# Statistics and pooled sums of the next image, done in three parts between the tap blocks instead of in one piece after them

## The chip, the cores and the metric

The program runs on one core of one Trainium2 chip. The metric is the device time of one execution in microseconds (us). The engines are PE (TensorE: matrix products and transposes), DVE (VectorE), ACT (ScalarE), POOL (GpSimd) and SP (SyncE, which issues the DMAs). Each engine works through its own queue in order; an instruction that must wait holds up everything behind it in that queue. PE writes its results to PSUM, in tiles named `ps`; ACT and DVE read them out.

## The reference

Four blocks follow one another on a batch x of 32 images with 192 channels of 56 by 56 points, in float32. Each normalises x over groups of 6 channels, applies a layer, and adds the result to x. Layer 0 is an agent attention, layer 1 a two-way recurrent scan, layer 2 a shifted 3 by 3 blur, and layer 3 a convolution as large as the image. The change lies in the kernel's attention stage, so layer 0 is what matters:

```python
qkv = xf @ Wqkv + bqkv                       # x normalised, all 3136 points
agent = qi.mean(axis=(2, 4))                 # q averaged over 8 by 8 points: 49 agents
agent_attn = softmax(ah * scale @ kh + pos_bias)      # over the points
agent_v = agent_attn @ vh
q_attn = softmax(qh * scale @ ah + agent_bias)        # over the 49 agents
out = q_attn @ agent_v + dwc(vh)             # dwc: a 3 by 3 convolution per channel
x = x + out @ proj_w + proj_b
```

The normalisation needs the mean and the variance of each group of channels over the whole image. The agents need only the sums of x over squares of 8 by 8 points, because the mean of q is a product of the mean of x.

## The kernel before

The program runs in stages. First a filter for layer 3 is made, up to about 230 us. Then the attention takes the images one after another, up to about 4850 us; the scan follows up to about 8200 us, and the channel stage (layers 2 and 3) ends the program.

An image is held as two tiles: `x[0]` has channels 0 to 127, with all 56 rows, and `x[1]` has channels 128 to 191, with the upper half of the rows on partitions 0 to 63 and the lower half on 64 to 127. Its points are cut into four blocks of columns, numbered 0 to 3, of 16, 16, 16 and 8 columns (`WIDTHS`). The attention of one image (from line 843) has two parts.

The first loop runs over the blocks j. `weigh(j)` multiplies the block with the agents' keys in three steps of two heads each; DVE takes the maximum of each (`low`, L664), ACT the exponential of it (`pr`, L666). `turn_v(j)` and `turn(j)` transpose the values and the weights on PE (L681, L694), and ACT copies the results (`vT` L682, `prT` L697). `gather(j - 1)` multiplies the turned weights of the block before with its values (L709), and `settle` turns and adds that block's result (L718 on PE, `got` L720 on ACT and L722 on DVE). `find_v(j + 2)` computes the values of a later block (L621 to L634). `convolve(j + 1)` computes the 3 by 3 convolution of the next block: ACT starts it (L647) and DVE adds eight taps for each of the two tiles (L649). Behind the last block, `moments` of the next image runs in the place of a convolution.

The second part starts with `ask(0)`: PE multiplies the first block with the agents' queries (L763, L764), DVE takes maxima (`mx`, L767) and subtracts them (`pq`, L768), ACT takes exponentials (L776), DVE sums and divides (L778 to L780). `join` (L727 to L742) merges the four blocks' softmaxes into `values`. The second loop, over t, asks for the other blocks, turns the weights back (L790), answers (L801, L806), projects (L921 to L934) and adds to x (L816, L822). Between these steps it prepares the next image: `spread_of` (with the matrix product L545) and `scaling` finish the statistics, `normed`, `find_v(0)`, `find_v(1)`, `find_agents`, `seen` and `convolve(0)` follow.

`moments` (L510 to L539) is all DVE work: seven `bn_stats` of `x[0]` (L515), four of `x[1]` (L517), two aggregates (L519, L520), sums over 8 columns of both tiles (`by_x`, L524), and sums over 8 rows (`pool_a` L527; `fours` L532 and `pool_c` L535).

The order of each engine's queue is not the order of the code. A planner takes the instructions of the program in the order in which they are written as their priority, follows a model of their durations, and puts into each engine's queue whatever can start by that model; so an instruction written early goes early, and later ones fill holes. `psum()` hands out four result tiles. The images lie in two buffers; the next image's load (L424, L426) is issued when the image before has been stored.

Of the kernel before, what the change touches and what calls it, by code (L numbers as in the profile page):

```python
# [23 lines left out]
ALU = mybir.AluOpType  # L24
AX = mybir.AxisListType
# [17 lines left out]
POOL = 7  # L43
# [396 lines left out]
def attention(ctx: ExitStack, tc: tile.TileContext, a, ready, x1, st_a, st_c, beside):  # L440
# [9 lines left out]
    nc = tc.nc  # L450
# [11 lines left out]
    def psum():  # L462
        return pp.tile([128, 2, BANK], F32, name="ps", tag="ps")
# [30 lines left out]
    def small(name, shape):  # L494
        return sp.tile(shape, F32, name=name, tag=name)
# [14 lines left out]
    def moments(x):  # L510

        st_a, st_c = small("st_a", [128, 7, 6]), small("st_c", [128, 4, 6])
        flat = [t.rearrange("p y x -> p (y x)") for t in x]
        for i in range(7):
            nc.vector.bn_stats(st_a[:, i], flat[0][:, i * 448 : (i + 1) * 448])  # L515
        for i in range(4):
            nc.vector.bn_stats(st_c[:, i], flat[1][:, i * 392 : (i + 1) * 392])  # L517
        mv = small("mv", [128, 2, 2])
        nc.vector.bn_aggr(mv[:, 0], st_a.rearrange("p a b -> p (a b)"))  # L519
        nc.vector.bn_aggr(mv[:, 1], st_c.rearrange("p a b -> p (a b)"))  # L520
        pool_a, pool_c = small("pool_a", [128, AG]), small("pool_c", [65, AG])
        by_x = [wp.tile([128, n, POOL], F32, name="by_x", tag=f"by_x{n}", bufs=1) for n in (S, S // 2)]
        for t in range(2):
            nc.vector.tensor_reduce(  # L524
                by_x[t].rearrange("p y q -> p (y q)"), x[t].rearrange("p y (q x) -> p (y q) x", x=8), AX.X, ALU.add
            )
        nc.vector.tensor_reduce(  # L527
            pool_a.rearrange("p (w q) -> p w q", w=POOL), by_x[0].rearrange("p (w y) q -> p w q y", y=8), AX.X, ALU.add
        )
        fours = small("fours", [64, 2 * POOL, POOL])  # L530
        for h, r in HALVES:
            nc.vector.tensor_reduce(  # L532
                fours[:, h * POOL : (h + 1) * POOL], by_x[1][r].rearrange("p (w y) q -> p w q y", y=4), AX.X, ALU.add
            )
        nc.vector.tensor_tensor(  # L535
            pool_c[0:64].rearrange("p (w q) -> p w q", w=POOL), fours[:, 0::2], fours[:, 1::2], ALU.add
        )
        nc.vector.memset(pool_c[64:65], 1.0)
        return mv, (pool_a, pool_c)  # L539

    def grouped(src):
        ps = psum()
# [5 lines left out]
    def spread_of(mv):  # L548

        mean = small("mean", [128, 2])  # L550
        nc.vector.tensor_copy(mean, grouped([mv[:, t, 0:1] for t in range(2)]))
        d = small("d", [128, 2])
        nc.vector.tensor_tensor(d, mv[:, :, 0], mean, ALU.subtract)
        nc.vector.tensor_tensor(d, d, d, ALU.mult)
        nc.vector.tensor_tensor(d, d, mv[:, :, 1], ALU.add)
        return mean, d

    def scaling(mean, d, pools):

        pool_a, pool_c = pools  # L560
        rs, nb = small("rs", [128, 2]), small("nb", [128, 2])
        nc.vector.tensor_scalar(rs, grouped([d[:, t : t + 1] for t in range(2)]), GN_EPS, None, ALU.add)
        nc.scalar.activation(rs, rs, AF.Ln)
        nc.scalar.activation(rs, rs, AF.Exp, scale=-0.5)
        nc.vector.scalar_tensor_tensor(nb, mean, -1.0, rs, ALU.mult, ALU.mult)
        rs64 = small("rs64", [128, 2])
        nc.vector.tensor_scalar(rs64, rs, 1.0 / (S // POOL) ** 2, None, ALU.mult)
        nc.vector.tensor_scalar(pool_a, pool_a, rs64[:, 0:1], nb[:, 0:1], ALU.mult, ALU.add)
        nc.vector.tensor_scalar(pool_c[0:64], pool_c[0:64], rs64[0:64, 1:2], nb[0:64, 1:2], ALU.mult, ALU.add)
        return rs, nb  # L570
# [83 lines left out]
    def weigh(j, g, low, sums):  # L654
        _, n, _ = sizes(j)
        prs = []
        for p in range(3):
            cols = slice(p * PAIR, (p + 1) * PAIR)
            ps = psum()
            for h in range(2):  # L660
                px = slice(h * n, (h + 1) * n)
                mm(ps[P2, h, :n], g[:, cols], xs_a[j][:, px], start=True, stop=False)  # L662
                mm(ps[P2, h, :n], gk_c[0:KC, 2 * j + h, cols], xs_c[j][0:KC, px], start=False, stop=True)  # L663
            nc.vector.tensor_reduce(low[:, j, p : p + 1], ps[P2, :, :n], AX.XY, ALU.max, negate=True)  # L664
            pr = wp.tile([PAIR, 2, CH], F32, name="pr", tag="weights", bufs=WB)
            nc.scalar.activation(  # L666
                pr[:, :, :n], ps[P2, :, :n], AF.Exp, bias=low[:, j, p : p + 1], accum_out=sums[:, j, p : p + 1]
            )
            prs.append(pr)
        return prs  # L670
# [43 lines left out]
    def settle(j, halves, got):  # L714

        ps = psum()
        for p in range(3):
            nc.tensor.transpose(ps[P2, 0, p * 128 : (p + 1) * 128], halves[:, p * PAIR : (p + 1) * PAIR], ident)  # L718
        both = ps[P2, 0, : 3 * 128].rearrange("p (a h d) -> p a h d", a=3, h=2)
        nc.scalar.copy(got[:, j].rearrange("p (a d) -> p a d", a=3), both[:, :, 0])  # L720
        mine = got[:, j].rearrange("p (a d) -> p a d", a=3)
        nc.vector.tensor_tensor(mine, mine, both[:, :, 1], ALU.add)  # L722
# [109 lines left out]
            )  # L832

    nxt = ready.first
    mv, pools = moments(nxt)
    rs, nb = scaling(*spread_of(mv), pools)
    ag = find_agents(0, pools)
    gk = seen(ag, wkT, gk_c, "gk_a")
# [4 lines left out]
    for b in range(NB):  # L843
        x, more = nxt, b + 1 < NB
        if more:
            nxt = ready.image(nc, a, b + 1)
        beside(b)
        low, sums = small("low", [PAIR, NK, 3]), small("sums", [PAIR, NK, 3])
        got = sp.tile([PAIR, NK, C], F32, name="got", tag="got", bufs=1)
        turned, asked, back = {}, {}, {}  # L850
        for j in range(NK):
            prs = weigh(j, gk, low, sums)
            if j == 0:
                gq = seen(ag, wqT, gq_c, "gq_a")
            vT = turn_v(j, v[j])
            if j > 0:
                halves = gather(j - 1, *turned[j - 1])
            if j + 2 < NK:
                v[j + 2] = find_v(j + 2)
            turned[j] = turn(j, prs), vT  # L860
            if j > 0:
                settle(j - 1, halves, got)
            if j + 1 < NK:
                o[j + 1] = convolve(j + 1)
            elif more:
                mv, pools = moments(nxt)
        halves = gather(NK - 1, *turned[NK - 1])
        asked[0] = ask(0, gq)
        settle(NK - 1, halves, got)
        values = join(low, sums, got)  # L870
        done, o = o, {}
        st = small("st", [128, 2, 9])
        for t in range(1, NK + 2):
            if t < NK:
                asked[t] = ask(t, gq)
            if more and t == 1:
                mean, d = spread_of(mv)
            if more and t == 2:
                rs, nb = scaling(mean, d, pools)
                normed(nxt, rs, nb, 0)  # L880
            if t <= NK:
                back[t - 1] = turn_back(t - 1, asked[t - 1])
            if more and t in (3, 4):
                v[t - 3] = find_v(t - 3)
            if t >= 2:
                project(t - 2, done[t - 2], x, st)
            if t <= NK:
                answer(t - 1, back[t - 1], values, done[t - 1])
            if more and t == 2:
                ag = find_agents(b + 1, pools)  # L890
                normed(nxt, rs, nb, 1)
            if more and t == 3:
                gk = seen(ag, wkT, gk_c, "gk_a")
                normed(nxt, rs, nb, 2)
            if more and t == 4:
                o[0] = convolve(0)
                normed(nxt, rs, nb, 3)
        nc.sync.dma_start(out=st_a[:, b % 2, b // 2], in_=st[:, 0])
        for h, r in HALVES:
            nc.sync.dma_start(out=st_c[b % 2, :, h, b // 2], in_=st[r, 1])  # L900
        nc.sync.dma_start(out=x1[b, 0:128], in_=x[0].rearrange("p y x -> p (y x)"))
        for h, r in HALVES:
            nc.sync.dma_start(
                out=x1[b, 128:C, 1568 * h : 1568 * h + 1568], in_=x[1][r].rearrange("p y x -> p (y x)")
            )
# [1094 lines left out]
```

## Time and profile before

| what | us |
|---|---|
| median of three runs | 10493.24 (10483.27 to 10510.5) |
| profiled execution: its time, its span | 10489.98, 10488.2 |
| PE busy over the span | 9430.8 (90%) |
| DVE busy | 9115.9 (87%) |
| ACT busy | 6351.2 (61%) |
| POOL busy | 2225.9 (21%) |
| mean granted PE clock | 0.963 of full speed |

A busy time counts the engine's own instructions, not the waits between them, and the share is an average over stages that have different limits. PE's busy times are modelled at their ends and overlap a little; the granted clock says what share of full speed PE was allowed. In a row of the timeline the first number is the start in us from the span's start and the second the length; `low<-ps` says that `low` is written from `ps`, `x2` counts instructions in the row, and `[2.88 <-PE ps L764]` says that the engine was idle for 2.88 us before it, until a PE instruction of line 764 released it. Lines are those of the kernel before.

### The profile page before, as it was taken

The page shows a single profiled execution, that of the slowest core. Times are in us where ns is not written, and L with a number is a line of the kernel's source. Part 1 is how long each engine was busy: PE and PEld are TensorE (multiplying, and loading weights), DVE is VectorE, ACT ScalarE, POOL GpSimd, SP SyncE. Part 2 cuts the span into 40 slices and gives each one's busy share as a digit, 9 for nine tenths or more (in the row PEclk, how much of TensorE's full clock was granted, in tenths as well). Part 3 has the DMA queues.
Part 4 walks back from the last instruction along what each step waited for, and adds up shares of the span by engine and source line. Part 5 has one row for each costly group of instructions (what it writes and reads, how often), then busy time and mean ns, then how long its engine had stood idle before and what let it go on. Part 6 is the DMA issues. An engine that isn't in the chain of part 4 may idle for free. (4 is left out here: it accounts for less than half of the span.)

```text
span 10488.2 us, 163343 instructions
## 1 busy us (share of the span) xinstructions
PE 9430.8 (90%) x63814; PEld 5820.0 (55%) x63814; DVE 9115.9 (87%) x11284; ACT 6351.2 (61%) x11964; POOL 2225.9 (21%) x1751
## 2 busy tenths in 40 slices
PE   5999999999999999998888888888888798999998
PEld 3556555555555555554333333433433587787776
DVE  5888888888888888887999999999999687888887
ACT  3555555555555555554666666666666476777776
POOL 0000000000000000000433333333333444444441
PEclk8999999999999999999899999999999899999999
DMA  4211222122211211011344444444444599999999
GB/s 127 67 42 59 67 67 66 37 65 67 67 49 52 67 49 49 27 46 57 87 106 101 100 100 102 104 104 105 106 100 102 145 285 273 286 292 284 281 286 281
DMA packets 1111098, 1247.63 MB, mean 119 GB/s; under 512 B 773091, under 2 KB 813440, under 8 KB 1098232
## 3 DMA queue, kind: packets, MB, share of 16 engines
q1 hardware_dynamic: 1089388, 1209.08, 40.6%
q10 hardware_dynamic: 20932, 28.02, 1.0%
q8 instruction: 507, 8.31, 0.3%
q14 instruction: 271, 2.22, 0.1%
HBM read 916.15 MB, written 306.43 MB: 117 GB/s over the span
## 5 line engine op out<-in xcount | busy, mean ns | idle before, releaser
L649 DVE SCALAR_TENSOR_TENSOR o<-v_a,att_w,o 128x896 f32<-128x896 f32 (+1 forms) x1024 | 1058.7, 1034 | 423.5 <-ACT v_a L623 303.3
L1167 POOL MEMSET f<- 128x2 f32 x48 | 4.5, 100 | 4738.4 <-DMA st_c<-st 4735.9
L1546 ACT COPY y<-ps 64x252 f32<-64x252 f32 (+1 forms) x2304 | 785.9, 341 | 105.9 <-PE ps L1546 76.3
L1546 DVE STREAM_TRANSPOSE z<-turned 128x1792 f32<-128x1792 f32 x192 | 677.1, 3527 | 161.9 <-ACT turned L1546 161.2
L1161 ACT ACTIVATE pq<-pq 128x784 f32<-128x784 f32 x384 | 330.0, 860 | 673.3 <-DVE pq L1157 673.0
L1157 DVE SCALAR_TENSOR_TENSOR pq<-both,eu,pq 128x1568 f32<-128x1568 f32 x384 | 702.2, 1843 | 2.0 <-POOL f L1156 0.4
L1153 DVE TENSOR_TENSOR_SCAN pq<-decay,f,both 128x784 f32<-128x784 f32 x384 | 695.8, 1841 | 8.4 <-ACT both L1183 8.4
L666 ACT ACTIVATE pr<-ps,low 98x896 f32<-98x896 f32 (+1 forms) x384 | 352.9, 919 | 572.0 <-DVE low L664 572.0
L1153 DVE TENSOR_TENSOR_SCAN pq<-decay,b,both 128x784 f32<-128x784 f32 x384 | 694.7, 1842 | 0.0
L921 PE MATMUL ps<-x,weights 128*128 128x392 f32 x1536 | 585.6, 520 | 90.3 <-ACT x L1141 63.7
L649 DVE SCALAR_TENSOR_TENSOR o<-v_c,att_w,o 128x448 f32<-128x448 f32 (+1 forms) x1024 | 640.1, 625 | 5.1
L662 PE MATMUL ps<-xs_a,gk_a 128*98 128x448 f32 (+1 forms) x1536 | 637.0, 496 | 0.0
L663 PE MATMUL ps<-xs_c,gk_c 125*98 125x448 f32 (+1 forms) x1536 | 631.2, 492 | 0.0
L776 ACT ACTIVATE pq<-pq 128x1176 f32<-128x1176 f32 (+2 forms) x224 | 242.3, 1082 | 634.2 <-DVE pq L768 612.2
L1141 ACT ACTIVATE x<-x,nb,rs 128x784 f32<-128x784 f32 x384 | 387.7, 1033 | 339.7 <-DMA x<-x 178.6
L763 PE MATMUL ps<-gq_a,xs_a 128*128 128x294 f32 (+1 forms) x1600 | 544.8, 423 | 37.7 <-DVE pq L768 33.1
L1546 PEld LDWEIGHTS ps<-toep,y 128*32 128x32 f32 x16896 | 500.4, 150 | 137.5 <-ACT y L1546 130.8
L1546 POOL TENSOR_TENSOR xn<-x,scale 128x896 f32<-128x896 f32 x192 | 327.2, 1704 | 1099.3 <-DMA x<-x 563.0
L1156 POOL COPY b<-pq 128x2 f32<-128x2 f32 x192 | 419.0, 2182 | 660.5 <-DVE pq L1153 567.1
L1546 PE MATMUL ps<-toep,y 128*32 128x112 f32 x16896 | 547.5, 285 | 2.0 <-DMA toep<-spans 2.0
L1546 PE MATMUL ps<-rows,xn 128*112 128x112 f32 x3072 | 366.6, 275 | 193.2 <-POOL xn L1546 192.2
L764 PE MATMUL ps<-gq_c,xs_c 125*128 125x294 f32 (+1 forms) x1600 | 517.8, 411 | 0.0
(360 smaller groups left out, 23528.0 us busy)
## 6 DMA issues: line engine op xcount, KB each, us to landing
toep<-spans SPq DMA_DIRECT2D x192, 2352.0 KB
x<-x SPq DMA_DIRECT2D x576, 392.0 KB
x<-x SPq DMA_DIRECT2D x896, 196.0 KB
out_x<-done SPq DMA_DIRECT2D x384, 196.0 KB
spans<-lags SPq DMA_DIRECT2D x24, 2352.0 KB
x<-in_x SPq DMA_DIRECT2D x32, 1568.0 KB
x<-x SPq DMA_DIRECT2D x32, 1568.0 KB
gq_c<-once SPq DMA_DIRECT2D x32, 821.1 KB
```

The source lines that it names most:

```text
L649: nc.vector.scalar_tensor_tensor(dst, tap(i), dww[:, t, i : i + 1], dst, ALU.mult, ALU.add)
L662: mm(ps[P2, h, :n], g[:, cols], xs_a[j][:, px], start=True, stop=False)
L663: mm(ps[P2, h, :n], gk_c[0:KC, 2 * j + h, cols], xs_c[j][0:KC, px], start=False, stop=True)
L666: nc.scalar.activation(pr[:, :, :n], ps[P2, :, :n], AF.Exp, bias=low[:, j, p : p + 1], accum_out=sums[:, j, p : p + 1])
L763: mm(ps[:m, k - q, :HA], xs_a[j][:, px], g, start=True, stop=False)
L764: mm(ps[:m, k - q, :HA], xs_c[j][0:KC, px], gq_c[0:KC, which[k]], start=False, stop=True)
L921: mm(out, aa, srcs[t][h], start=True, stop=False)
L1141: nc.scalar.activation(xs[t], xs[t], AF.Identity, bias=nb1[:, t, s.p : s.p + 1], scale=rs1[:, t, s.p : s.p + 1])
L1153: nc.vector.tensor_tensor_scan(to, decay[:, of(t)].to_broadcast([128, MC]), data, at[:, i : i + 1], ALU.mult, ALU.add)
L1156: nc.gpsimd.tensor_copy(at, z[:, :, last])
L1157: nc.vector.scalar_tensor_tensor(before, both, eu[:, of(t)], before, ALU.mult, ALU.add)
L1546: return lambda *args, **kw: self.tc.keep_in_program_order(do(*args, **kw))
```

## The change

`moments` becomes a generator with three parts, and the image loop takes one part at a time. The first part holds the seven `bn_stats` of `x[0]`. The second holds the four of `x[1]`, both aggregates, and the pooled sums of `x[1]` (small `by_x`, `fours`, `pool_c`). The third holds the pooled sums of `x[0]` (large `by_x`, `pool_a`). For j = 1, 2 and 3 one part is written behind block j's `settle(j - 1)` and ahead of `convolve(j + 1)`, where there is one. At j = 0 the generator is only made and nothing runs. For the first image, before the loop, all parts run at once as before. The instructions are the same ones; in the last image, which has no successor, there are none, as before.

```diff
         for i in range(7):
             nc.vector.bn_stats(st_a[:, i], flat[0][:, i * 448 : (i + 1) * 448])
+        yield
         for i in range(4):
             nc.vector.bn_stats(st_c[:, i], flat[1][:, i * 392 : (i + 1) * 392])
...
-        for t in range(2):
+
+        def by_column(t):
             nc.vector.tensor_reduce(
                 by_x[t].rearrange("p y q -> p (y q)"), x[t].rearrange("p y (q x) -> p (y q) x", x=8), AX.X, ALU.add
             )
-        nc.vector.tensor_reduce(
-            pool_a.rearrange("p (w q) -> p w q", w=POOL), by_x[0].rearrange("p (w y) q -> p w q y", y=8), AX.X, ALU.add
-        )
+
+        by_column(1)
         fours = small("fours", [64, 2 * POOL, POOL])
...
         nc.vector.memset(pool_c[64:65], 1.0)
-        return mv, (pool_a, pool_c)
+        yield
+        by_column(0)
+        nc.vector.tensor_reduce(
+            pool_a.rearrange("p (w q) -> p w q", w=POOL), by_x[0].rearrange("p (w y) q -> p w q y", y=8), AX.X, ALU.add
+        )
+        yield mv, (pool_a, pool_c)
...
     nxt = ready.first
-    mv, pools = moments(nxt)
+    *_, (mv, pools) = moments(nxt)
...
             if j > 0:
                 settle(j - 1, halves, got)
+            if more and j == 0:
+                parts = moments(nxt)
+            elif more:
+                found = next(parts)
             if j + 1 < NK:
                 o[j + 1] = convolve(j + 1)
-            elif more:
-                mv, pools = moments(nxt)
+        if more:
+            mv, pools = found
         halves = gather(NK - 1, *turned[NK - 1])
```

## The prediction

> **What bounds the kernel now.** I read the page first.
>
> ```profile
> PE 9430.8 (90%) x63814; PEld 5820.0 (55%) x63814; DVE 9115.9 (87%) x11284; ACT 6351.2 (61%) x11964; POOL 2225.9 (21%) x1751
> ```
>
> PE and DVE are both close to full, so the average decides nothing; the change touches the attention stage alone, and the question is who waits there. I marked the images by their one `values` product (L742). From image 2 to image 24 these stand at 419.24 and 3655.82 us: 22 images of 147.12 us. Next I cut one image into stretches (columns: stretch, its length, then the busy time and instructions of PE, PEld, DVE, ACT, POOL, granted clock, DMA share, GB/s).
>
> ```profile
> 2392.14:2539.50 147.36, 138.74 (x786) 85.71 (x785) 124.59 (x194) 80.32 (x146) 0.00 (x0) 0.98 0.19 60
> 2414.50:2456.50 42.00, 41.40 (x306) 28.13 (x304) 41.83 (x61) 25.87 (x52) 0.00 (x0) 1.00 0.29 92
> 2456.50:2468.10 11.60, 11.40 (x108) 8.61 (x105) 11.27 (x23) 3.54 (x9) 0.00 (x0) 1.00 0.01 1
> 2468.10:2489.00 20.90, 14.74 (x67) 11.63 (x67) 20.38 (x31) 5.46 (x7) 0.00 (x0) 0.84 0.00 0
> ```
>
> The image as a whole is PE's (8.6 us idle), but from 2414.5 to 2489 DVE hardly pauses (73.5 of 74.5 us busy): this is the stretch of the taps, the maxima, the statistics and the first queries, and DVE sets its length. PE's largest wait stands in it, in the answer on PE's waits in this image (us in total, times, longest):
>
> ```profile
> PE ps L545 <- DVE pq L768: 4.5, 1, 4.5
> ```
>
> So whatever makes DVE idle between 2414.5 and 2489 lengthens the image by as much, and moving DVE work about inside the stretch gains nothing by itself. Now DVE in order of time, where the moved work stands (start, length, instruction):
>
> ```profile
> 2455.94 0.63 DVE L664 TENSOR_REDUCE low<-ps 98x1 f32<-98x448 f32 x1
> 2456.46 1.16 DVE L515 BATCH_NORM_STATS2 st_a<-x 128x6 f32<-128x448 f32 x2
> 2457.52 1.97 DVE L517 BATCH_NORM_STATS2 st_c<-x 128x6 f32<-128x392 f32 x4
> 2459.39 0.35 DVE L519 BATCH_NORM_AGGREGATE mv<-st_a 128x2 f32<-128x42 f32 x1
> 2459.64 0.23 DVE L520 BATCH_NORM_AGGREGATE mv<-st_c 128x2 f32<-128x24 f32 x1
> 2459.76 3.38 DVE L524 TENSOR_REDUCE by_x<-x 128x392 f32<-128x3136 f32 x1
> 2463.04 0.36 DVE L722 TENSOR_TENSOR got<-got,ps 98x192 f32<-98x192 f32 x1
> 2463.29 1.80 DVE L524 TENSOR_REDUCE by_x<-x 128x196 f32<-128x1568 f32 x1
> 2464.99 0.86 DVE L527 TENSOR_REDUCE pool_a<-by_x 128x49 f32<-128x392 f32 x1
> 2465.75 0.98 DVE L532 TENSOR_REDUCE fours<-by_x 64x49 f32<-64x196 f32 x2
> 2466.77 0.17 DVE L727 TENSOR_REDUCE m<-low 98x3 f32<-98x12 f32 x1
> ...
> 2468.12 0.76 DVE L767 TENSOR_REDUCE mx<-ps 128x12 f32<-128x588 f32 x1
> ```
>
> The first row is the image's last maximum, which ends at 2456.57; the last row is the first query's first maximum. Between them lie 11.55 us of DVE work, most of it `moments`. PE needs part of that time: after the last `low`, ACT takes the exponentials, PE turns them, gathers, and multiplies the first query. PE in the same order of time:
>
> ```profile
> 2465.05 1.15 PE L764 MATMUL ps<-gq_c,xs_c 125*128 125x294 f32 x4
> ```
>
> The first query's tile is complete with the first half of this row, at 2465.71 (.66 after its start, as in the single rows of L764). DVE comes at 2468.12. So the statistics cover PE's path from the last maximum to the first query, 9.14 us, with 2.4 us to spare.
>
> **The change, part by part.** No instruction is added or removed and no DMA moves; SP's and POOL's orders are the same. On DVE the built program puts all seven `st_a` after the last maximum of block 1 (three stood four taps later, four among the last maxima), then four `st_c`, both aggregates, the small `by_x`, `fours` and `pool_c` after the last maximum of block 2, and leaves only the large `by_x` and `pool_a` behind the last maximum of block 3. PE and ACT change in the last two blocks only: ACT takes `vT` ahead of a block's first exponential, and PE sets settle 2 between the fourth and the fifth transpose of block 3.
>
> 1. Work moved ahead of the last maximum, by start-to-start times above: two `st_a` 1.06, four `st_c` 1.87, aggregates .37, small `by_x` 1.70, `fours` 1.02: 6.02 us. Inside DVE's full stretch this costs and gains nothing.
>
> 2. What DVE has left between the last maximum and the first query: large `by_x` 3.28, `got` .25, `pool_a` .76, the join's small chain 1.35 (2466.77 to 2468.12), less .11 by which the maximum's row overlaps the next: 5.53 us (5.53 + 6.02 = 11.55, as measured).
>
> 3. What the path over ACT and PE then takes. The last image has no `moments`, and shows it bare:
>
> ```profile
> 4811.57 0.62 DVE L664 TENSOR_REDUCE low<-ps 98x1 f32<-98x448 f32 x1 [0.52 <-PE ps L663]
> ...
> 4819.73 0.77 DVE L767 TENSOR_REDUCE mx<-ps 128x12 f32<-128x588 f32 x1 [2.88 <-PE ps L764]
> ```
> ```profile
> 4812.12 2.24 PE L709 MATMUL ps<-prT,vT 112*64 112x98 f32 x48
> ```
>
> From the maximum's end (4812.19) to the end of the second L764 (4819.69) there are 7.50 us, and DVE idled 2.88 us there before its `mx`. That path still held gather 2 (the 2.24 us row). After the change the last maximum comes about 6 us later, when gather 2 is past. I rebuild the path: .10 to the exponential (4812.29), .73 for it with its sum (to 4813.02), .41 for the first four of the eight transposes still open (the .75 from L694's start at 4814.30 to the copy at 4815.05, less four times .084), .73 from the copy to the gather (4815.05 to 4815.78), 3.91 from the first gather to the second L764's end (to 4819.69), and 1.00 for two more L763 that stand ahead of it in the changed order (.50 each): 6.88, and .04 to DVE's start: 6.92 us. DVE has 5.53 us of work for it. It will wait 1.39 us, in every one of the 31 images that have a successor: 43 us. From below: with nothing but the last image less gather 2 the path is 7.50 - 2.24 = 5.26, under 5.53, and the wait is 0. From above: the path of the image before, 9.14 - 5.53 = 3.6 us, 112 us in all. I take 1.39, since it uses the changed order row by row.
>
> 4. The wait of L545 remains: after the first query's `mx` DVE's order is what it was, and PE still needs DVE to free one of its four result tiles. So the clock loss after it remains too. Whole images took 146.71, 147.63 and 148.29 us at a mean clock of .99, .98 and .97: about .8 us for each further stretch of 3.41 us at half clock. An image of 147.1 us is 43.1 such stretches, so a lucky place in the grid repeats; one of 148.5 us is 43.5 and wanders over all places. The mean loss is now 1.5 stretches ((147.12 - 146.71) / .8 + 1), and should be nearer 2: .3 us, 9 us in all. Bounds: -.4 and +.8 us an image, one half stretch less or one more.
>
> 5. Landing of the next image. The first `st_a` moves from 2430.87 to about 2427; the loads of x are issued at 2405.01 and 2408.86, and from 2428 to 2430 the DMA share is .08. No DVE wait stands before `st_a` now; I cost it at 0 because x's loads are ahead of the 2.4 MB copy of spans in the same queue. If the cover is gone it costs DVE the lateness, at most 3 us.
>
> 6. The later maxima let PE and ACT idle in blocks 2 and 3 (some 4 us of PE in pieces of up to 1.2 us). DVE is behind them and does not feel it; its cost is in step 3.
>
> Sum: 43 + 9 = 52 us on the profiled execution's own 10490.0 us (span 10488.2): 10542. The median of the runs is 10493.2, 3 us above that execution.
>
> A rule against the change stands in the Trainium skill, "TensorE: Matmul & The Clock Gate", Part 4: transposes do not count as PE work for the clock as matmuls do. The row:
>
> ```profile
> 2484.95:2488.37 3.42, 3.42 (x18) 3.25 (x16) 3.40 (x6) 1.31 (x2) 0.00 (x0) 0.50 0.00 0
> 2488.37:2491.78 3.41, 3.41 (x18) 1.38 (x17) 2.23 (x4) 2.14 (x3) 0.00 (x0) 1.00 0.03 7
> ```
>
> In the first of these stretches PE did L790 transposes alone, and the clock rose to full after it, so here they count. By the rule the sparse 4 us of block 3's transposes would halve the clock in every image: 1.7 us each, 53 us more, 10595. By the row it stays.
>
> **Rivals.**
> - The path is hidden anyway (wait under .5 us). For it: 5.26 us, step 3's lower bound. Against: the last image's DVE, with no statistics at all, waits. 10490 + 0 to 24: 10490 to 10514, within .3%.
> - The clock falls in block 3 as well. PE would be busy about half of a 3.41 us stretch there. In this trace it fell after a stretch with 1.42 us of PE work (4102.88 to 4106.29) and held after one with 1.79 (2467.89 to 2471.30); half of 3.41 is 1.7. The first query would run at half clock: 1.7 us an image more, 10595.
> - Faster: DVE idles 5.88 us (2408.6 to 2414.49) before block 1's taps for `v_a`. If the seven `st_a` (3.7 us) ran in that hole, DVE would be 3.7 us early, L545's wait would shrink to .8 and most of the clock loss of 1.2 go: 31 x 4.9 = 152 us, 10338. It decides whether `st_a` stands before the first tap of block 1 in the DVE queue. It stands behind block 1's last maximum, so this is nearly excluded.
>
> **How the numbers follow.** A measurement tells about .3% (31 us) from no change. Chances: the forecast (wait of .5 to 2.7 us) .72, hidden .12, clock .12, faster .04. The time is the first's: 10542; its own range is 10505 (.5 us) to 10589 (2.7 us and half a stretch of clock). The range for 8 in 10 is this one, a little into the clock's case: 10505 to 10592. Slower by over .3% than the median means above 10525, a loss of 1.1 us an image: most of the forecast (.62) and the clock's case (.12): .74. Same: the rest of the forecast (.10) and hidden (.12): .22. Faster .04.
>
> **What would show it.** Right: DVE waits 1 to 2 us at the first L767 after the join, ended by PE L764, in each image; L545's wait of 4 us stays; image length about 148.8 us; scan and channel stages as before. Wrong: no such wait, with the join directly followed by `mx` (step 3); a DVE wait at `st_a` for a DMA (step 5); clock .50 in the stretch of block 3's transposes (step 4 and the rule).

## The result

The kernel after takes 10617.33 us (median of 4 runs, 10614.19 to 10621.25), the kernel before on the same chip 10493.01 us (median of 4, 10483.27 to 10510.5). The ratio is 1.0114, with a 95% interval of 1.0101 to 1.0127: by it 120 us more (124 by the medians). The forecast was 10542 with a range of 10505 to 10592; the direction was right, and the loss is more than twice the 52 us forecast. The profiled execution of after took 10614.19 us, with a span of 10612.4.

All of it lies in the attention. From the first `values` product to the last (31 images) before took 4560.4 us and after 4688.0: 127.6 us more, against 124.2 between the two spans. Images in the middle took about 147.2 us before; now they alternate between 151.34 and 152.4.

The lines named here have moved by 6: L664 is now L670, L694 is L700, L709 is L715, L718 is L724, L763 and L764 are L769 and L770, the first `mx` is L773, and L545 is L551. Within `moments` the large `by_x` is now L526 and `pool_a` L542.

First the engines' busy times on the page, and DVE in order of time from the last maximum of an image to its first query:

```profile
PE 9512.0 (90%) x63814; PEld 5888.9 (55%) x63814; DVE 9131.2 (86%) x11284; ACT 6331.5 (60%) x11964; POOL 2197.0 (21%) x1751
```
```profile
2526.46 0.62 DVE L670 TENSOR_REDUCE low<-ps 98x1 f32<-98x448 f32 x1
2526.99 3.42 DVE L526 TENSOR_REDUCE by_x<-x 128x392 f32<-128x3136 f32 x1
2530.32 0.35 DVE L728 TENSOR_TENSOR got<-got,ps 98x192 f32<-98x192 f32 x1
2530.58 0.85 DVE L542 TENSOR_REDUCE pool_a<-by_x 128x49 f32<-128x392 f32 x1
...
2533.84 0.17 DVE L737 TENSOR_TENSOR sums<-sums,f 98x12 f32<-98x12 f32 x1 [1.97 <-ACT f L736]
...
2537.69 0.77 DVE L773 TENSOR_REDUCE mx<-ps 128x12 f32<-128x588 f32 x1 [3.06 <-PE ps L770]
```

The counts are those of before: nothing was added. PE is 81 us busier with the same 63814 instructions, so some of them ran slower. On DVE the work between the last maximum (it ends at 2527.08) and `mx` is 10.61 - 1.97 - 3.06 = 5.58 us, where the forecast had 5.53. But DVE now waits 5.0 us there in this image and 3.5 us in its neighbour, where 1.39 us were forecast and before has .1. Where does the rest of the wait come from? The stretches (columns as in the prediction: length, then busy time and instructions of PE, PEld, DVE, ACT, POOL, granted clock, DMA share, GB/s) show it:

```profile
2397.75:2550.09 152.34, 142.24 (x785) 88.20 (x785) 124.84 (x195) 79.88 (x145) 0.00 (x0) 0.96 0.19 58
2525.51:2528.92 3.41, 2.19 (x15) 1.41 (x15) 3.41 (x5) 2.89 (x9) 0.00 (x0) 1.00 0.00 0
2528.92:2532.33 3.41, 3.15 (x20) 2.14 (x22) 2.85 (x6) 0.76 (x2) 0.00 (x0) 0.50 0.02 5
2532.33:2535.74 3.41, 3.41 (x15) 2.41 (x12) 0.69 (x4) 0.52 (x2) 0.00 (x0) 0.50 0.00 0
```

The clock falls to half at 2528.92, just as PE begins the last gather and the first query, and stays there for two stretches. That is the path DVE is waiting for. PE in order of time shows what preceded the fall:

```profile
2526.11 0.59 PE L700 MATMUL ps<-att_k,pr 98*112 98x98 f32 x2 [1.39 <-ACT pr L672]
2527.03 0.38 PE L700 MATMUL ps<-att_k,pr 98*112 98x98 f32 x2 [0.33 <-ACT pr L672]
2527.25 0.49 PE L724 MATMUL ps<-att_k,halves 128*98 128x128 f32 x3
2527.90 0.89 PE L700 MATMUL ps<-att_k,pr 98*112 98x98 f32 x8 [0.15 <-ACT pr L672]
2529.18 0.59 PE L715 MATMUL ps<-prT,vT 112*64 112x98 f32 x2 [0.40 <-ACT prT L703]
2529.70 1.35 PE L769 MATMUL ps<-gq_a,xs_a 128*128 128x294 f32 x2
```

Block 3's transposes come in pairs, each behind an exponential, and each exponential behind a maximum that DVE now reaches later. Over the 31 images the clock record of the trace has 28 falls here with 150.2 us at half clock; before has none. The other fall, behind the wait of the statistics' product (L545 before, L551 now), is there in all 31 images of both, with 201.4 us at half clock in each. PE's waits in this image (us in total, times, longest) still have it:

```profile
PE ps L551 <- DVE pq L774: 4.2, 1, 4.2
PE ps L700 <- ACT pr L672: 1.9, 3, 1.4
```

So there are two candidates for the 120 us: the cover on DVE is too short for the path (theory of the forecast), and the clock falls on that path (the forecast's second rival).

### The profile page after: what moved, and what is told of

Read it like the earlier page. It is cut to its first block, busy times and chain, and to the rows that moved or that the text cites. A ratio compares the mean times of both kernels' runs of the same rounds, so it can differ in the third digit from the quotient of the medians.

```text
span 10612.4 us, 163297 instructions
## 1 busy us (share of the span) xinstructions
PE 9512.0 (90%) x63814; PEld 5888.9 (55%) x63814; DVE 9131.2 (86%) x11284; ACT 6331.5 (60%) x11964; POOL 2197.0 (21%) x1751
## 5 line engine op out<-in xcount | busy, mean ns | idle before, releaser
L769 PE MATMUL ps<-gq_a,xs_a 128*128 128x294 f32 (+1 forms) x1600 | 563.5, 440 | 0.0
L770 PE MATMUL ps<-gq_c,xs_c 125*128 125x294 f32 (+1 forms) x1600 | 518.2, 412 | 0.0
```

What stands on the lines that cost most here:

```text
L769: mm(ps[:m, k - q, :HA], xs_a[j][:, px], g, start=True, stop=False)
L770: mm(ps[:m, k - q, :HA], xs_c[j][0:KC, px], gq_c[0:KC, which[k]], start=False, stop=True)
```

## The experiments

Theory A: both are at work, and they add: a short cover costs what the path at full clock exceeds it by, and the fall of the clock costs about as much again. Rival B: the short cover alone explains the loss, and the half clock only accompanies it. Rival C: moving the work to its new places costs by itself, through blocks 1 to 3.

### Keeping PE busy in block 3

Six products of the identity with itself, into columns of the result tile that nothing reads, stand in front of block 3's transposes. Line numbers behind them are 3 higher.

```diff
-    def turn(j, prs):
+    def turn(j, prs, busy=False):
...
             ps = psum()
+            if busy and q == 0:
+                for _ in range(6):
+                    mm(ps[:, 0, 320:448], ident, ident, start=True, stop=True)
...
-            turned[j] = turn(j, prs), vT
+            turned[j] = turn(j, prs, more and j == NK - 1), vT
```

> The changed kernel with six extra matrix products (identity by identity, into unused columns of the result tile) written ahead of block 3's transposes, so that PE has about 1.3 us of work in the stretch where it waits for the last exponentials. The extra products are not part of the computation. Theory A (the clock): the changed kernel loses about 3 of its 4 us an image because PE's clock falls to half in that stretch; with PE busy there the clock stays at 1.00, the second L770 ends about 7 us after the last maximum, DVE waits 1 to 1.5 us, an image takes 148.5 us and the whole 10530 to 10560 us. Theory B (the path itself): the path over ACT and PE is simply longer than rebuilt, because ACT's order changed; then the extra work adds to it and the time is 10617 us or more.

Measured: 10553.82 us (10542.89 to 10576.39), 1.0056 (1.0038 to 1.0074) of before's 10498.0 in the same comparison. No fall in block 3 in any image. With more work on PE the program is .0058, or 61 us, faster than after: this part of the loss is the clock, and B falls. The stretches, then DVE and PE in order of time (the first PE row is the extra products: a product is two instructions there, and they run behind the wait of 1.39 us for block 3's first exponential):

```profile
2496.89:2500.30 3.41, 3.12 (x30) 2.77 (x30) 3.41 (x3) 2.47 (x7) 0.00 (x0) 1.00 0.00 0
2500.30:2503.71 3.41, 3.41 (x32) 2.55 (x32) 2.78 (x10) 0.89 (x4) 0.00 (x0) 1.00 0.00 0
```
```profile
2497.06 0.62 DVE L670 TENSOR_REDUCE low<-ps 98x1 f32<-98x448 f32 x1
...
2502.82 0.17 DVE L740 TENSOR_TENSOR sums<-sums,f 98x12 f32<-98x12 f32 x1 [0.33 <-ACT f L739]
...
2505.39 0.77 DVE L776 TENSOR_REDUCE mx<-ps 128x12 f32<-128x588 f32 x1 [1.78 <-PE ps L773]
```
```profile
2496.71 1.60 PE L699 MATMUL ps<-att_k 128*128 128x128 f32 x12 [1.39 <-ACT pr L672]
...
2499.95 0.38 PE L718 MATMUL ps<-prT,vT 112*64 112x98 f32 x2 [0.29 <-ACT prT L706]
2500.26 0.76 PE L772 MATMUL ps<-gq_a,xs_a 128*128 128x294 f32 x2
2500.95 1.22 PE L718 MATMUL ps<-prT,vT 112*64 112x98 f32 x22
2502.11 1.75 PE L772 MATMUL ps<-gq_a,xs_a 128*128 128x294 f32 x6
2503.70 0.66 PE L773 MATMUL ps<-gq_c,xs_c 125*128 125x294 f32 x2
2504.20 0.66 PE L772 MATMUL ps<-gq_a,xs_a 128*128 128x294 f32 x2
2504.69 1.15 PE L773 MATMUL ps<-gq_c,xs_c 125*128 125x294 f32 x4
```

Here the forecast's own mechanism stands alone, at full clock. From the gather on PE's order is the same as in after; there 22 instructions of the gather (L715) took 2.22 us at half clock, here (L718) 1.22. The last maximum ends at 2497.68 and the second L773 at 2505.35: a path of 7.67 us, and DVE waits .33 + 1.78 = 2.1 us, where 1 to 1.5 were expected. In the last seven images that have a successor three pairs of L772 fewer stand ahead of the second L773; there the path is 6.18 us, and the wait .6. In the very first image no `moments` stands there in either kernel (the planner has put the second image's ahead of the attention, up to 178 us), and its wait of 2.87 us is in both. So 23 images lose 2.1 us and seven lose .6, 53 us in all; the remaining loss of .0056 is 56 us by the medians.

### How much work is left behind the last maximum

Four kernels differ from after only in where the generator's pauses stand. The first leaves only the seven `st_a` early, and all else in one piece where it was before.

```diff
         for i in range(7):
             nc.vector.bn_stats(st_a[:, i], flat[0][:, i * 448 : (i + 1) * 448])
         yield
+        yield
...
         nc.vector.memset(pool_c[64:65], 1.0)
-        yield
         by_column(0)
```

> Only the first part (seven st_a) is moved ahead; the rest of moments stays in one piece behind block 3. DVE then has 11.55 - 1.06 = 10.5 us of work between the last maximum and the first query. Theory A and B (cover): still more than PE's path of 9.1 us, no DVE wait, no fall of the clock in block 3: 10493 us, within .3%. Theory C (the first part itself costs, by delaying block 2's maxima by 2.1 us): a share of the loss, 10530 us or more.

Measured: 10472.0 us, .9976 (.9965 to .9987). The next has all statistics early and all pooled sums last:

```diff
+        yield
         by_column(1)
...
         nc.vector.memset(pool_c[64:65], 1.0)
-        yield
         by_column(0)
```

> The statistics of both tiles stand early, as in the changed kernel; all pooled sums stay behind block 3. DVE has 5.53 + 1.70 + 1.02 = 8.25 us between the last maximum and the first query. Theory A: at full clock the path takes 7 us and is hidden, the time is 10493 us within .3%; if the clock falls in block 3 all the same (the last maximum comes 3.3 us later than before), the path of 9.1 to 10.6 us shows 1 to 2.4 us of DVE wait in those images, up to 10560 us. Theory B (a path of 9.1 us or more at any clock): a wait of about 1 us, 10520 us.

Measured: 10474.7 us, .9974 (.9963 to .9984). DVE keeps 8.3 us of work behind the last maximum, and `mx` waits for nothing:

```profile
2466.44 0.17 DVE L737 TENSOR_TENSOR sums<-sums,f 98x12 f32<-98x12 f32 x1 [0.28 <-ACT f L736]
...
2467.14 0.76 DVE L773 TENSOR_REDUCE mx<-ps 128x12 f32<-128x588 f32 x1
```

Both have 0 falls in block 3, both take moved work at no cost, and both are slightly faster than before; so C falls for the statistics (the pooled sums of `x[1]` weren't moved alone). What decides is not that work was moved ahead, but how much was left. The gain of some 25 us isn't explained; a part may be the half clock behind the wait of the statistics' product, which is 188 and 154 us in these two where before has 201. The third leaves none of it:

```diff
         nc.vector.memset(pool_c[64:65], 1.0)
-        yield
         by_column(0)
...
+        yield
         yield mv, (pool_a, pool_c)
```

> The third part stands with the second, so that nothing of moments is left behind block 3's last maximum; DVE has 5.53 - 3.28 - .76 = 1.5 us there. All theories that speak of cover: 4.0 us more of DVE wait than in the changed kernel, 31 x 4.0 = 124 us more, about 10740 us, with a clock that falls in every image. If the loss came from the moved parts delaying block 2 and 3 alone, without the cover, it would stay near 10617 us.

Measured: 10760.87 us, 1.0257 (1.0233 to 1.028), close to the 10740 expected. Images take 157.0 us, DVE waits .5 + 1.8 + 6.9 us, and the clock falls in 30 images, in most for three stretches, 300 us in all. The fourth holds part 1 back to the place of part 2, so that the work behind the last maximum is the same as in after:

```diff
         flat = [t.rearrange("p y x -> p (y x)") for t in x]
+        yield
         for i in range(7):
             nc.vector.bn_stats(st_a[:, i], flat[0][:, i * 448 : (i + 1) * 448])
-        yield
```

> The changed kernel with its first part undone: the seven st_a stand with the second part, behind block 2's settle 1, instead of ahead of block 2's taps. DVE still has 5.53 us between the last maximum and the first query. Theory A (too little cover, then the clock): the same loss as the changed kernel, 10600 to 10630 us. Theory C (the first part carries a share): 10580 us or less.

Measured: 10655.47 us, 1.0162 (1.0137 to 1.0188) of before's 10488.6. That missed every expectation: the same cover, and 49 us worse than after. The stretches say why:

```profile
2543.12:2546.53 3.41, 1.16 (x28) 0.96 (x24) 3.41 (x8) 0.64 (x2) 0.00 (x0) 1.00 0.00 0
2546.53:2549.94 3.41, 2.55 (x13) 2.23 (x14) 3.41 (x4) 2.22 (x8) 0.00 (x0) 0.50 0.00 0
2549.94:2553.35 3.41, 3.33 (x20) 2.00 (x20) 2.44 (x6) 1.23 (x2) 0.00 (x0) 0.50 0.02 5
```

The planner put four of part 1's `st_a` behind block 2's last maximum, ahead of the last taps, and PE waits 2.79 us for block 3's first exponential where after has 1.39. It has only 1.16 us of work in the stretch before the transposes, and the clock falls 1.15 us before the last maximum ends (2547.68) instead of 1.8 us behind it. It falls in 30 images, in most for three stretches: 294 us at half clock instead of 150. This reading makes a forecast: take the clock's fall out of these two kernels, and what is left is the cover.

### The same extra products in these two

First the same six products in the kernel with part 1 held, and in the one with nothing left.

> The kernel with part 1 held to the place of part 2, plus the six extra products (not part of the computation) in front of block 3's transposes. Theory A (a short cover and a clock that falls in block 3 are the two causes, and the held part only lets the clock fall earlier): no fall of the clock in block 3, the wait at the first mx about 2.1 us as in the kernel after with the same products, and the time of that one: 10554, 10535 to 10575. Rival (the later place of part 1 costs something by itself, for instance a later chain in blocks 1 to 3): the clock stays up, but the time stays above 10600.

> The kernel with all seven statistics and all sums ahead of the last maximum, plus the six extra products (not part of the computation) in front of block 3's transposes. Theory A: no fall of the clock in block 3; the large by_x and pool_a (4.04 us) are missing from the cover, so DVE waits about 2.1 + 4.0 = 6.1 us an image between the last maximum and the first mx, 4.0 x 31 = 125 us above 10554: 10680, 10650 to 10710. Rival (once the clock stays up, PE's path is nearly hidden by other work and the cover costs little): under 10620.

Measured: 10604.98 us, 1.0108 (1.0078 to 1.0137) and 10786.14 us, 1.0281 (1.0251 to 1.0312), of before's 10495.89. Both missed their expectations, and neither settles the question, because the products ran too early. PE in the first kernel (an image that fell) and in the second:

```profile
2664.59 1.60 PE L699 MATMUL ps<-att_k 128*128 128x128 f32 x12 [0.56 <-ACT halves L720]
2666.82 0.38 PE L703 MATMUL ps<-att_k,pr 98*112 98x98 f32 x2 [0.63 <-ACT pr L672]
2667.72 0.38 PE L703 MATMUL ps<-att_k,pr 98*112 98x98 f32 x2 [0.52 <-ACT pr L672]
```
```profile
2598.80 1.60 PE L699 MATMUL ps<-att_k 128*128 128x128 f32 x12 [0.56 <-ACT halves L720]
2604.36 1.19 PE L703 MATMUL ps<-att_k,pr 98*112 98x98 f32 x4 [3.96 <-ACT pr L672]
```

In after with its products, these had waited for the same exponential as the transposes (the row of L699 above), and kept PE busy from there on; here they wait for an earlier copy (`halves`), run, and leave the gap. The first kernel's clock still falls in 15 images (75 us), the second's in 30 (300 us). The first kernel does show something: its images that kept the clock take 149.5 us, those with a fall 151.6 or 152.9. So the number of products was raised to fill the gaps: 11 and 21 in place of 6.

> As the kernel with part 1 held and six extra products, but with 11 of them (not part of the computation): the six ran ahead of two gaps of .63 and .52 us, and the clock still fell in 15 images, which took 151 to 153 us, while those in which it stayed took 149.5. Theory A: no fall in block 3, all images about 149.5, 10554 (10535 to 10575). Rival (the held part costs by itself): the clock stays and the time stays above 10600.

> As the kernel with all statistics and sums ahead of the last maximum and six extra products, but with 21 of them (not part of the computation): the six ran from 2598.80 to 2600.40 and left PE idle for 3.96 us before block 3's transposes, and the clock fell all the same; 15 more at .27 us fill that gap. Theory A (cover and clock are two separate losses): no fall of the clock in block 3; the path goes at full clock, about 8.3 us from the last maximum to the first mx instead of 10.9; the time falls by 2.6 us an image to about 10700, 10675 to 10725, which is the loss by the short cover alone. Rival (the clock's share was small and the length follows something else): 10750 or more with the clock at 1.00 there.

Measured: 10561.38 us, 1.0055 (1.0038 to 1.0072) with part 1 held, and 10687.57 us, 1.0165 (1.0148 to 1.0182) with nothing left, of before's 10508.31. The falls in block 3 are 0 and 3. Both times lie where theory A expected them; the three falls it did not expect. With part 1 held the ratio is that of after with its products, 1.0056: the extra loss of that kernel was the clock, and its place costs nothing. With nothing left the path at full clock is again 7.67 us, and DVE waits for nearly all of it:

```profile
2561.03 0.17 DVE L740 TENSOR_TENSOR sums<-sums,f 98x12 f32<-98x12 f32 x1 [0.49 <-ACT f L739]
...
2567.67 0.77 DVE L776 TENSOR_REDUCE mx<-ps 128x12 f32<-128x588 f32 x1 [5.59 <-PE ps L773]
```

The wait is 6.1 us where after with its products had 2.1; 4.0 us in each of 30 images, 120 us, were to be expected between the two, and the ratios differ by .0109, or 114 us.

Together (work is what DVE has left between the last maximum and `mx`; the waits are those of a middle image; half clock is the sum of the falls in block 3):

| kernel | work, us | waits, us | half clock, us | ratio to before |
|---|---|---|---|---|
| before | 11.4 | .1 | 0 | 1 |
| `st_a` alone early | 10.5 | .3 | 0 | .9976 |
| statistics early, sums last | 8.3 | .3 | 0 | .9974 |
| after, with products | 5.6 | 2.1 | 0 | 1.0056 |
| part 1 held, with 11 products | 5.6 | 2.0 | 0 | 1.0055 |
| after | 5.6 | 3.5 and 5.0 | 150 | 1.0114 |
| part 1 held | 5.6 | 5.6 | 294 | 1.0162 |
| none left, with 21 products | 1.6 | 6.1 | 14 | 1.0165 |
| none left | 1.7 | 9.2 | 300 | 1.0257 |

With 8.3 us of work left the path (7.83 us there) is hidden. With less than the path (7.67 in after with products) DVE waits for the difference, and with PE waiting for DVE's maxima the clock falls on top of that. The three pairs of kernels with and without falls agree on a price: 61 us for 150 us at half clock, 112 for 294 and 97 for 287, .34 to .41 us for each. How the 120 us divide is less certain than that there are two losses: measured from the kernel with 8.3 us left (.9974) instead of from before, the short cover would cost .0082, or 86 us.

### The wait that is in before too

The other fall of the clock follows the wait of L545. Ten of the same products behind the last L764 of the second block's query fill a part of that wait in before (lines behind them are 3 higher):

```diff
-    def ask(j, g):
+    def ask(j, g, busy=0):
...
+                if busy and u == n:
+                    for _ in range(busy):
+                        mm(ps[:, 0, 320:448], ident, ident, start=True, stop=True)
...
-                asked[t] = ask(t, gq)
+                asked[t] = ask(t, gq, 10 if more and t == 1 else 0)
```

> The kernel before with ten extra matrix products (identity by identity, into unused columns of the last result tile) behind the last L764 of the second query, so that PE has about 2.2 of its 4.5 us of waiting ahead of L545 filled. They are not part of the computation. Theory A: the half clock after that wait costs 1.2 us an image (147.1 against 145.9 without it); with the wait broken up the clock stays, an image takes 145.9 us and the whole 10450 to 10465 us. Rival: the clock is not what the wait costs, since PE has to wait for DVE anyway: 10493 us, or more by what the extra products add.

Measured: 10465.74 us, .9973 (.996 to .9986); the time at half clock goes from 201 to 120 us. That time is at the upper edge of the 10450 to 10465 expected, though for these the clock was to stay up. The wait is shorter and the clock still falls, for one stretch in most images:

```profile
PE ps L545 <- DVE pq L771: 2.3, 1, 2.3
```
```profile
2481.03:2484.44 3.41, 2.58 (x22) 2.33 (x20) 3.41 (x6) 0.00 (x0) 0.00 (x0) 1.00 0.00 0
2484.44:2487.85 3.41, 1.84 (x15) 1.61 (x15) 3.41 (x6) 1.23 (x2) 0.00 (x0) 1.00 0.00 0
2487.85:2491.27 3.42, 2.94 (x14) 2.68 (x14) 3.40 (x6) 2.06 (x3) 0.00 (x0) 0.50 0.00 0
```

The same edit to the kernel with the statistics early and the sums last, and to the one with `st_a` alone early:

> Statistics early and pooled sums last, with the ten extra products of the run before. Theory A: the image of 146.7 us loses its one stretch at half clock, .8 us or a little more: 10435 to 10450 us. Rival: no gain over 10475 us.

> The first part early, the rest last, with the ten extra products. Theory A: images 1 to 23 at 147.5 us lose two stretches at half clock, 1.5 us each time: 10472 - 35 = 10437 us; images 24 to 30 keep their 143.2 us. Rival: no gain over 10472 us.

Measured: 10461.26 us, .9972 (.9961 to .9983), nothing beyond the kernel without the products, so the expectation missed; and 10446.66 us, .9962 (.9946 to .9978). The median is near the 10437 expected, but mostly because before ran 9 us faster in this comparison: against the same kernel without products (.9976) the gain is 15 us by the ratios, not the 35 expected, and the intervals overlap. It has the lowest median of all, 42 us under before's 10488.6. Why its images 25 to 30 are shorter (143.1 us in most, where before has 145 to 149) wasn't followed up; they are so without the products too.

## Why the prediction was wrong, and where it was right

**Step 1 (moved work costs nothing): right.** The last maximum came 5.6 us later in the images shown (129.3 us behind the `values` product instead of 123.7) for 6.02 us of work, and the kernels with only `st_a` or all statistics early lose nothing.

**Step 2 (5.53 us left): right.** 5.58 measured.

**Step 3 (path of 6.92 us, wait of 1.39, 43 us): the mechanism was right, the path too short by .79 us.** At full clock it is 7.71 to the start of `mx`. Two terms were mis-sized. The transposes were put at .41 us, as four in a row; in the kernel with the products the copy came .81 us behind the exponential (it ends at 2498.44). And 1.00 us was allowed for two more pairs of L763; there are three, and gather to second query took 5.40 us, not 4.91. With an exponential of .76 for .83 and a gather of .70 for .73 this is .40 + .49 - .07 - .03 = .79. The wait is 2.1 us, and the cost 56 us. The copies, in after and in the kernel with products:

```profile
2528.48 1.20 ACT L703 COPY prT<-ps 112x588 f32<-112x588 f32 x2 [0.38 <-PE ps L700]
2499.25 1.20 ACT L706 COPY prT<-ps 112x588 f32<-112x588 f32 x2 [0.80 <-PE ps L703]
```

In after the exponential ends at 2527.84, and at a clock still full the copy came .64 us behind it. So .17 of the .81 belongs to the products, which pushed two transposes of settle 2 into that path; without them the path would be about 7.50 us (an estimate: 7.67 - .17), the cover's share some 5 us smaller and the clock's as much larger. The forecast also charged all 31 images; the first has the same wait before and after, and the last seven at full clock only .6 us. And the upper end of its own range, 10589, adds up from the median 10493, while the forecast starts at 10490.

**Step 4 (L545's wait stays): right, but the .3 us an image on top was not there.** Half clock behind that wait is 201.4 us before and after.

**Step 5 (landing): right.** No wait stands at `st_a`.

**Step 6 is the step that failed**: "The later maxima let PE and ACT idle in blocks 2 and 3 (some 4 us of PE in pieces of up to 1.2 us). DVE is behind them and does not feel it". The pieces are there (1.39, .33, .15 and .40 us), but DVE feels them through the clock, which stood at half for 150 us in 28 images: 61 us, half of the whole loss. With it fails the choice "By the row it stays". That row showed that a stretch without a pause, all transposes, brings the clock back. It could not tell how few of them keep it up, and that was the question.

**The rivals.** The one with the clock had the place and the mechanism, and its price of 1.7 us an image (53 us) is near the 61 measured; its time of 10595 is 22 us below the 10617 measured; 12 of these come from the sum it adds to (52 for 56) and from its own part (53 for 61), and the rest wasn't taken apart. It had a chance of .12, though the prediction's own numbers put PE's work in that stretch at the edge: it had held after 1.79 us, fallen after 1.42, and half a stretch is 1.7. At an edge it deserved about half. That it named the loss was partly luck: by its own measure, busy time, the 2.19 us of the stretch in after lie above the 1.79 that held, and the clock fell. The hidden path fails: even at full clock DVE waits. The faster one fails too: `st_a` did not move into the hole before block 1's taps.

The page "TensorE: Matmul & The Clock Gate" of the Trainium skill, in Part 4, says that transposes don't count as PE work for the clock in the same way. The sum by that rule, 10595, was nearer the result than the forecast, but no run here shows its reason. Two stretches held nothing but transposes and paused in between. One is in after, quoted above: 12 L700 and 3 L724, 2.19 us busy, and the clock fell behind it. The other is late in the kernel before with ten products, where it stayed:

```profile
4539.30:4542.72 3.42, 1.61 (x13) 1.11 (x11) 3.42 (x4) 1.97 (x3) 0.00 (x0) 1.00 0.00 0
4542.72:4546.13 3.41, 2.23 (x15) 1.29 (x17) 3.31 (x9) 1.36 (x3) 0.00 (x0) 1.00 0.00 0
```
```profile
4540.94 0.97 PE L793 MATMUL ps<-att_k,pq 128*98 128x128 f32 x7 [1.00 <-ACT pqT L795]
```

So transposes can hold the clock, and the busy time is not the measure of it. In the profile each small group of PE instructions carries a modelled tail: two L700 stand as .38 us, while in a row they follow one another every .084 us (L724 and L793 every .11). By that spacing the stretch that fell has 12 x .084 + 3 x .11 = 1.34 us of work and the one that held 13 x .11 = 1.43. That would explain the miss (the sparse stretch held less work than its busy time says), but it was only argued, and it isn't a clean limit: other stretches of after with 1.5 us by this count fell, and stretches of before with 1.3 us of query products held.

## What to carry to other kernels

Work on one engine that lies between two steps of another is a cover: before part of it is moved away, follow the path under it instruction by instruction, in the changed order, and leave at least that much. When an engine's late results thin out PE's work, cost the clock as a second loss of its own, because it strikes just the path that has lost its cover. A few extra products in the gap tell the two losses apart; see in the trace that they ran in the gap.

## What the runs showed of the hardware that was not expected

**In some kernels the length of an image settles on whole multiples of the clock's stretch.** A stretch is 3.413 us in the clock record. Images of several kernels came out alike to a few hundredths: 146.77 us, or 43 stretches (before with ten products, and its two variants); 153.6, or 45 (part 1 held; nothing left with 21 products); 157.0, or 46 (nothing left). In after two images together make 303.8 us, or 89, and with part 1 held and six products three make 454.0, or 133. The clock falls at a border of the grid, so the place of a wait in the grid sets how much half clock an image gets, and that sets the place in the next image; this explanation wasn't tested. Not every kernel settles: in before and in after with its products the length goes on changing from image to image. It bears on what a fix can bring: ten products that took 2.2 us off L545's wait in every image left the images at 146.77 us, where before's are at 147.2, and the second kernel that had them stood at 146.7 without them.

**Extra work made the program faster**, four times: 61 us in after (six products), 112 us with part 1 held (11), 97 us with nothing left (21), each by the difference of the two ratios, and 23 us in before (ten), by the medians.
